# Four graph layers on one core: the memsets between the gathers of layer 0 are taken out

## The chip, the cores and the metric

The kernel runs on one core of one Trainium2 chip. The metric is the device time of one execution in microseconds, the median of several. A profile of one execution lies beside it. A core has engines that run at the same time: TensorE (PE) for matmuls, VectorE (DVE), ScalarE (ACT), GpSimd (POOL) and SyncE (SP), and 16 DMA engines [...].

## The reference

A feature matrix x of 2708 x 512 float32 and an adjacency matrix adj of 2708 x 2708 pass through four layers. Few entries of adj are nonzero: the chance of an edge falls with the row and column number, and the diagonal is set. Every layer ends in a residual and a layernorm. Cut to what matters:

```python
# layer 0: degree-normalised graph convolution
adj_hat = adj + eye
d = 1 / sqrt(adj_hat.sum(axis=1))
x = layernorm(x + (d[:, None] * adj_hat * d[None, :]) @ x @ W.T + b)
# layer 1: adjacency plus a normalised 0/1 mask of it
mask = adj > 0
head = mask / max(sqrt(sum(mask * mask, axis=-1)), eps)
inc = adj + head
x = layernorm(x + (inc @ x) / inc.sum(axis=-1))
# layer 2: attention over the neighbours, gated
# layer 3: x = layernorm(x + relu(adj @ ((x > 0) @ sign(weight).T)))
```

## The kernel before

The function that does the work is `sparse_layers`. Rows are handled in 22 blocks of 128 (the last has 20). Block 0 has neighbours nearly everywhere and uses all of its adjacency row block; every other block uses a few column blocks directly ("direct" tiles) and, for the rest, gathers just those rows that are its neighbours.

The stages, by time in the profile, are these. From 0 to about 187 us the search reads adj, lists the neighbours of every block, packs the adjacency entries (the tiles `a`, fetched by indirect DMA at L1093) and computes y = x W0^T (L1127), which goes to DRAM as `y_rows`. Layer 0 runs from about 187 to 359 us, layer 1 to about 565, layer 2 to about 860 and layer 3 to the end.

Layer 0 is the loop at L1481 over `sequence`, which is 0, 1, 21, 2, 3, ... 20. For a block b it does this:

- DVE adds the bias b0 to the old features (L1486).
- For each gathered tile, `gathered` (L624) issues an indirect DMA on GpSimd (L626) that fetches up to 128 rows of `y_rows` into a buffer `xg`; the pool `s_l0` has ten of them. There are 98 such gathers in the layer.
- PE adds each tile's product with the packed adjacency into a PSUM tile `l0_b` (`add_tile`, L1393). A product of 128x512 float32 shows as two records in the trace. The PSUM pool of these tiles has two buffers.
- `grow1` adds one finished block, the one two places back in the sequence, into block 0's sum for layer 1: two DVE operations build `inc` (L1450, L1453; two buffers), and one matmul (L1454) adds it to `sum1`.
- DVE computes t = sum * dinv + old (L1508), and `layernorm` follows: statistics at L688 to L692, a square root on ACT (L663), Newton steps on DVE (L674 to L683), the normalised row at L704.
- SP writes the block to `x1_rows` in DRAM (L1512), from which layer 1 gathers.

Between the blocks lie side tasks for layer 1: `count_positive` counts positive entries of each block with small matmuls (L1183 to L1187), and `head_steps` turns the counts into the head's values (L1207 to L1226), which are spread by PE transposes (L1231) and copied by ACT (L1239). Blocks are counted in groups, such as 12, 13 and 14.

Layer 1 (from L1640) has the same form and gathers from `x1_rows` through the same function; its first incidence tiles are built at L1674. The search's own gathers have fills of another tile, `s_rest` (L1099), inside a block of code whose order is pinned.

After every third gather of layer 0 and every second of layer 1, `gathered` sets the tile `s_idle` (128x384 float32) to zero on GpSimd (L636). Nothing reads that tile. The table that turns this on is `pause`, keyed by the name of the DRAM tensor. For a tensor in the table, `behind` also adds a dependency without a semaphore from each gather or memset to the one before it, so that the scheduler keeps them in the order of the source. Outside of such pins and of the pinned block of the search, the order of instructions on each engine is set by the scheduler of the kernel language, from the data dependencies and its own costs.

Of the kernel before, what the change touches and what calls it, by code (L numbers as in the profile page):

```python
# [507 lines left out]
def sparse_layers(ctx, tc, x, adj, adj_t, w0_t, b0, w_sa, a_sa, w_gcnb, b_gcnb, wa, ba, wb, bb, w3_t,  # L508
# [56 lines left out]
    y_rows = dram.tile([PAD + P, D], F32, tag="y_rows", name="y_rows")  # L565
    x1_rows = dram.tile([PAD + P, D], F32, tag="x1_rows", name="x1_rows")
# [769 lines left out]
    head_row = heads.tile([P, N], F32, name="s_head_row")  # L1336
    wsa = heads.tile([P, KC, D + EXTRA], F32, name="s_wsa")
    idle = heads.tile([P, 384], F32, name="s_idle")
    for d, every in ((y_rows, 3), (x1_rows, 2)):
        pause[d.tensor.name] = (every, idle)  # L1340
    work = ctx.enter_context(tc.tile_pool(name="s_work", bufs=2, side="right", reuse_waits="tile"))

# [813 lines left out]
def kernel(  # L2156
# [25 lines left out]
    flag = ctx.enter_context(tc.tile_pool(name="flag", bufs=1))  # L2182
    over = flag.tile([1, 1], I32, name="over")
    sparse_layers(tc, *args, over)
    n_over = nc.values_load(over[0:1, 0:1], min_val=0, max_val=-(-x.shape[0] // P))
    with tc.If(n_over > 0):
# [43 lines left out]
```

## Time and profile before

| what | us |
|---|---|
| median of 3 runs | 988.28 |
| lowest, highest | 986.34, 994.11 |
| the profiled execution | 992.0 |
| its span | 990.3 |
| PE busy in the span | 860.8 |
| POOL busy in the span | 549.4 |

The mean granted clock of PE was 0.946 in the profiled execution. The span runs from the first to the last instruction on the core. "Busy" counts work, not waiting or issuing. In a group's line, the part before the bar names source line, engine, operation, output and inputs and count; after the bar stand the busy time, the mean of one in ns, and the idle time of the engine just before them with what ended most of it. Idle time of an engine that others don't wait for costs nothing.

### The profile page before, as it was taken

The page shows a single profiled execution, that of the slowest core. Times are in us where ns is not written, and L with a number is a line of the kernel's source. Part 1 is how long each engine was busy: PE and PEld are TensorE (multiplying, and loading weights), DVE is VectorE, ACT ScalarE, POOL GpSimd, SP SyncE. Part 2 cuts the span into 40 slices and gives each one's busy share as a digit, 9 for nine tenths or more (in the row PEclk, how much of TensorE's full clock was granted, in tenths as well). Part 3 has the DMA queues.
Part 4 walks back from the last instruction along what each step waited for, and adds up shares of the span by engine and source line. Part 5 has one row for each costly group of instructions (what it writes and reads, how often), then busy time and mean ns, then how long its engine had stood idle before and what let it go on. Part 6 is the DMA issues. An engine that isn't in the chain of part 4 may idle for free.

```text
span 990.3 us, 12880 instructions
## 1 busy us (share of the span) xinstructions
PE 860.8 (87%) x3659; PEld 452.2 (46%) x3659; DVE 654.7 (66%) x2538; ACT 381.1 (38%) x822; POOL 549.4 (55%) x660
## 2 busy tenths in 40 slices
PE   1898789759979979999999989988999999599992
PEld 0444344212222324555555634543555555378771
DVE  4888888726657766565654446675888776556685
ACT  2665556100000014554544433333444333254653
POOL 2577888687877647776542054553454320066661
PEclk9998998979989989999999998998999999889996
DMA  9999996466777646777653276786777541299985
GB/s 266 339 336 306 301 310 199 142 193 192 237 211 222 207 132 195 223 220 233 183 176 121 97 249 236 257 276 216 249 274 261 174 149 47 85 316 331 308 249 173
DMA packets 93557, 220.06 MB, mean 222 GB/s; under 512 B 13660, under 2 KB 28364, under 8 KB 93476
## 3 DMA queue, kind: packets, MB, share of 16 engines
q0 software_dynamic: 43008, 127.61, 43.5%
q1 hardware_dynamic: 38520, 76.78, 22.6%
q10 hardware_dynamic: 11948, 14.76, 4.7%
q8 instruction: 31, 0.51, 0.2%
q14 instruction: 50, 0.41, 0.1%
HBM read 178.21 MB, written 31.71 MB: 212 GB/s over the span
## 4 chain that ended last, share of the span: by engine, by line
PE 68%; DVE 14%; DMA 7%; issue 5%; ACT 2%; another core or an unknown queue 2%; POOL 1%; SPq 0%; ACTq 0%; DVEq 0%; POOLq 0%
PE l L1393 17%; PE h L1619 8%; PE e L1844 7%; PE a L1844 7%; PE l L2099 4%; PE pg L1892 4%; PE pc L1892 3%; PE y L1127 3%; PE l L2138 2%; PE l L1454 2%; PE e L1652 2%; PE a L1653 2%; PE px L1953 2%; DVE s_mask L895 2%; DMA xg<-x_rows,i 2%
## 5 line engine op out<-in xcount | busy, mean ns | idle before, releaser
L1093 POOL DMA_INDIRECT a<-in_adj_t_dram,row_at x98 | 111.3, 1136 | 58.7 <-DVE deg L838 26.1
L626 POOL DMA_INDIRECT xg<-x_rows,i x98 | 95.8, 978 | 70.7 <-PE l L1393 37.1
L626 POOL DMA_INDIRECT xg<-y_rows,i x98 | 97.7, 997 | 32.6 <-issue 19.0
L1393 PE MATMUL l<-xg,a 128*32 128x512 f32 (+3 forms) x196 | 86.0, 646 | 12.6 <-DMA xg<-y_rows,i 12.6
L1820 POOL DMA_INDIRECT xg<-x_rows,i x60 | 59.1, 986 | 61.8 <-ACT ae L1575 16.3
L1127 PE MATMUL y<-s_w,xt 128*128 128x512 f32 (+1 forms) x176 | 91.3, 667 | 1.7 <-ACT xt L1119 1.7
L626 POOL DMA_INDIRECT xg<-xw_rows,i x70 | 71.3, 1018 | 38.7 <-issue 15.9
L1820 POOL DMA_INDIRECT a<-x_rows,i x38 | 36.9, 970 | 95.1 <-DVE mask L1578 37.1
L1619 PE MATMUL h<-s_wsa,xt 128*128 128x256 f32 (+3 forms) x352 | 81.9, 385 | 0.0
L1619 PEld LDWEIGHTS h<-s_wsa,xt 128*128 128x128 f32 (+1 forms) x352 | 63.9, 186 | 24.8 <-ACT xt L1614 9.2
L830 ACT ACTIVATE unused<-arow 128x1408 uint8<-128x1408 f32 (+3 forms) x44 | 58.3, 1325 | 3.0 <-DMA x_rows<-s_zero 2.0
L663 ACT ACTIVATE rsqs<-mv 128x1 f32<-128x1 f32 (+2 forms) x56 | 11.3, 202 | 120.7 <-DVE mv L692 58.8
L1844 PE MATMUL a<-xg,a 128*32 128x512 f32 (+2 forms) x120 | 51.2, 629 | 4.3 <-DMA xg<-x_rows,i 4.3
L1127 PEld LDWEIGHTS y<-s_w,xt 128*128 128x128 f32 (+1 forms) x176 | 35.6, 213 | 41.9 <-issue 39.6
L2099 PE MATMUL l<-ws,pw 128*128 128x512 f32 (+1 forms) x210 | 50.8, 394 | 1.7 <-issue 1.2
L1844 PE MATMUL e<-xg,ae 128*32 128x512 f32 (+2 forms) x120 | 47.9, 601 | 1.1 <-issue 1.1
L694 POOL TENSOR_TENSOR rs<-mv,s_neg_half 128x1 f32<-128x1 f32 (+1 forms) x22 | 13.0, 592 | 61.4 <-DVE mv L692 52.0
L1892 PE MATMUL pg<-s_wg,pt 128*128 128x256 f32 (+1 forms) x176 | 45.0, 397 | 1.3 <-ACT pt L1880 1.3
L688 DVE BATCH_NORM_STATS2 st<-t 128x6 f32<-128x512 f32 (+1 forms) x66 | 45.3, 687 | 0.3
L916 PE MATMUL find<-s_sides,s_mask 128*128 128x5 bf16 (+1 forms) x462 | 15.7, 166 | 34.1 <-DVE s_mask L912 25.2
L2099 PEld LDWEIGHTS l<-ws,pw 128*128 128x128 f32 (+1 forms) x210 | 39.4, 190 | 11.9 <-issue 2.9
L1393 PEld LDWEIGHTS l<-xg,a 128*32 128x32 f32 (+3 forms) x196 | 19.8, 146 | 54.4 <-issue 38.6
(307 smaller groups left out, 1995.5 us busy)
## 6 DMA issues: line engine op xcount, KB each, us to landing
arow<-in_adj_dram SPq DMA_DIRECT2D x21, 704.0 KB
arow<-in_adj_dram SPq DMA_DIRECT2D x21, 650.0 KB
x_rows<-f SPq DMA_DIRECT2D x40, 256.0 KB
aw<-in_adj_t_dram SPq DMA_DIRECT2D x21, 320.0 KB
y_rows<-yt ACTq DMA_DIRECT2D x20, 256.0 KB
x_rows<-h SPq DMA_DIRECT2D x19, 257.0 KB
f<-in_x_dram SPq DMA_DIRECT2D x19, 256.0 KB
h_own<-x_rows SPq DMA_DIRECT2D x19, 256.0 KB
```

The costliest lines, as they stand in the source:

```text
L626: nc.gpsimd.indirect_dma_start(out=t, out_offset=None, in_=src[:, :], in_offset=bass.IndirectOffsetOnAxis(ap=index[b][:, i : i + 1], axis=0),)
L688: nc.vector.bn_stats(st[:m], t[:m])
L830: nc.scalar.activation(unused[:m, : ar.shape[1]], ar, AF.Copy, accum_out=row_sums[:m, b, h : h + 1])
L895: nc.vector.tensor_scalar(mask[:m, c0 : c0 + ar.shape[1]], ar, 0.0, None, op0=ALU.not_equal)
L1093: nc.gpsimd.indirect_dma_start(out=packed[b][:, t + len(direct(b)), :], out_offset=None, in_=adj_t, in_offset=bass.IndirectOffsetOnAxis(ap ...
L1127: nc.tensor.matmul(ps[:m], xt[:, k, :m], w0[:, k, :], start=(k == 0), stop=(k == KC - 1))
L1393: nc.tensor.matmul(ps[r0:r1], weights, moving, start=(i == order[0]), stop=last_of(b, i, order))
L1619: nc.tensor.matmul(ps, xt[:, k, :m], w[:, k, :], start=(k == 0), stop=(k == KC - 1))
L1820: nc.gpsimd.indirect_dma_start(out=g, out_offset=None, in_=x2_rows[:, :], in_offset=bass.IndirectOffsetOnAxis(ap=index[b][:, t : t + 1], a ...
L1844: nc.tensor.matmul(ps[r0:r1], weights, moving, start=(i == order[0]), stop=last_of(b, i, order))
L1892: nc.tensor.matmul(ps, pt[:, k, :m], w[:, k, :], start=(k == 0), stop=(k == KC - 1))
L2099: nc.tensor.matmul(whole[b], p[:r, h, b * P : (b + 1) * P], g[:r, :], start=(j == 0 and h == 0), stop=(j == NB - 1 and h == 1),)
```

## The change

One entry of the table goes. The gathers of `y_rows` are then no longer followed by memsets, and they are no longer pinned to each other. The 49 memsets of layer 1 and the 43 of the search stay, and so does the pin on layer 1's gathers.

```diff
     idle = heads.tile([P, 384], F32, name="s_idle")
-    for d, every in ((y_rows, 3), (x1_rows, 2)):
+    for d, every in ((x1_rows, 2),):
         pause[d.tensor.name] = (every, idle)
```

The rest of the program's text is the same. 32 memsets of layer 0 leave the program; the gathers keep their number, their sizes and their buffers.

## The prediction

> **What bounds the kernel now.** I began with the page, to see which engine carries the whole:
>
> ```profile
> span 990.3 us, 12880 instructions
> PE 860.8 (87%) x3659; PEld 452.2 (46%) x3659; DVE 654.7 (66%) x2538; ACT 381.1 (38%) x822; POOL 549.4 (55%) x660
> PE 68%; DVE 14%; DMA 7%; issue 5%; ACT 2%; another core or an unknown queue 2%; POOL 1%; SPq 0%; ACTq 0%; DVEq 0%; POOLq 0%
> L626 POOL DMA_INDIRECT xg<-y_rows,i x98 | 97.7, 997 | 32.6 <-issue 19.0
> ```
>
> The profiled execution took 992.0 us, 1.7 more than its span. TensorE is busy 87% and holds 68% of the chain that ended last; GpSimd, whose work the change takes out, holds 1%. The last line is layer 0's 98 gathers of y rows, which all run on GpSimd. An average says little of one stage, so I cut out layer 0 (196 to 356 us) and asked for the stretch, its chain and its waits:
>
> ```profile
> 196.00:356.00 160.00, 132.56 (x404) 39.27 (x404) 100.40 (x448) 10.28 (x41) 115.28 (x133) 0.90 0.68 203
> ```
>
> The columns are length, then busy time of PE, weight load, DVE, ACT and POOL, then PE clock, DMA share, GB/s. POOL is at 72% (115.28 of 160), PE at 83%, and the DMA engines at 0.68 are not full.
>
> ```profile
> by line: PE l L1393 60.5%; PE l L1454 13.1%; issue 6.3%; DMA xg<-y_rows,i 3.2%; PE hr L1187 2.9%; PE hr L1231 2.6%; DVE t L1508 1.9%; POOL a L1093 1.7%; another core or an unknown queue 1.4%; DVE st L688 1.1%; DVE pos L1185 1.1%; DVE f L704
> ```
>
> In layer 0 too the chain is PE's matmuls (60.5 + 13.1 + 2.9 + 2.6 = 79%). The gathers' transfer is 3.2%, and L626 or L636 on POOL do not appear in the line. The waits (total us, times, longest) say who stands still for whom:
>
> ```profile
> POOL xg L626 <- issue: 19.0, 76, 0.3
> ...
> PE l L1393 <- DMA xg<-y_rows,i: 12.6, 1, 12.6
> ...
> POOL xg L626 <- PE l L1393: 8.7, 13, 2.2
> ...
> PE l L1454 <- DVE t L1508: 4.4, 1, 4.4
> ...
> PE l L1454 <- DVE rsqs L682: 2.3, 1, 2.3
> ```
>
> PE waited for a gather once, for the first one; 97 gathers were there in time. POOL, in turn, waited 13 times for PE to give back one of the ten xg buffers. So GpSimd runs ahead of PE, is stopped by it, and is mostly cover. What stops PE inside the stage is DVE: the sums that `grow1` adds for layer 1 need a normalised block (L1508 to L704).
>
> [...] a gather holds POOL 0.947 us, so fills and gathers share one engine's time. [...] A few gathers take 1.02 to 1.15 us, [...] Here the records of one 128x512 matmul take 0.857 us after a wait (x2 in 2.07 us at 282.79) and 0.427 us otherwise, [...]
>
> **The change part by part.** *The fills.* 32 memsets of s_idle (L636; 15.0 us by the group list, 467 ns each) go. The POOL timeline gives what one costs:
>
> ```profile
> 203.80 0.95 POOL L626 DMA_INDIRECT xg<-y_rows,i  x1 [0.16 <-issue]
> 205.06 0.95 POOL L626 DMA_INDIRECT xg<-y_rows,i  x1 [0.30 <-issue]
> 206.31 0.95 POOL L626 DMA_INDIRECT xg<-y_rows,i  x1 [0.30 <-issue]
> 207.26 0.43 POOL L636 MEMSET s_idle<- 128x384 f32 x1
> 207.85 0.94 POOL L626 DMA_INDIRECT xg<-y_rows,i  x1 [0.16 <-issue]
> ```
>
> Three gathers and a fill take 207.85 − 203.80 = 4.05 us; without the fill they take 3 × 1.25 (206.31 − 205.06) = 3.75 us. A fill costs POOL 0.30 us net, since it sits where a 0.30 us gap would be anyway. 32 × 0.30 = 9.6 us is all that POOL can win, of the 145 us between its first gather (199.6) and its last (344.5).
>
> What of it is on the path? PE's work in the stage is 98 gathered tiles, 18 direct ones and 21 sums, 137 × 2 records × 0.427 = 117 us, and some 9 us of counts and transposes (L1187, L1231). It takes from 204.9 to about 352, so some 21 us are waits and half speed, and only the start is owed to gathers. The first nine gathers contain two fills ahead of tiles that PE takes as they land: 2 × 0.30 = −0.6 us. The other 30 shorten a lead that POOL already has, and POOL turns the time into waiting for buffers. Layer 1 gains nothing there: its first gather needs the last x1 rows written, and POOL stands idle 14.65 us before it.
>
> *The order.* `behind` also fixed the gathers' order for the scheduler. Comparing the order of both programs by engine: gathers and SP's queue come in the same order, and layers 1 to 3 are the same; PE, DVE and ACT are re-sorted inside layer 0. No instruction is added and no new wait. Gather matmuls move ahead of the sums and counts. Step by step:
> - `grow1` of block 1 gets one more matmul (0.86 us) ahead of it, where PE waited 2.3 us for L682: −0.86. `grow1` of block 7 gets three more (2.6 us) where PE waited 4.4 us for L1508: −2.6. Together −3.4.
> - PE ran 2.6 us longer than its work after that second wait, at half speed (282.8 to 288.6). Whether 1.8 us of rest still slows it I can't tell: bounds 0 and −2.6, I take the half, −1.3.
> - The head transposes of blocks 12 to 14 lose cover: four matmuls lie between the last count and them instead of seven (3 × 0.86): +2.6 at most, and I take that, as PE already waited 1.2 us at one such place (L1231 on hd).
> - At the tail the last norm comes seven DVE instructions later, some 0.15 us each: +1.0. One more `grow1` is left for the end; it lies beside the last x1 write and gather, so nothing, and 0.86 us if that cover is gone.
> - DVE's t of two blocks now come in pairs before their norms. Elsewhere PE has 10 to 14 us between a block's last matmul and its sum, 7 to 9 before. More cover: nothing now, since those places didn't wait.
>
> Sum: −0.6 − 3.4 − 1.3 + 2.6 + 1.0 = −1.7 us. The profiled 992.0 becomes 990.3; it stood 3.7 above the median, and I put the difference on the median: 988.28 − 1.7 = 986.6.
>
> **The rivals.**
> *A, POOL paces after all (faster).* If the lead is only apparent, the full 9.6 us come off in place of 0.6: −10.7, 977.6. For: 19.0 us of POOL's idle time is its own issue gap, and PE used the first nine tiles, and again about ten near 260 to 277 us, only 5 to 6.5 us after their issue, when a transfer lands 3.0 to 4.2 us after it. Against: one wait for a gather, 13 for buffers.
>
> *B, the fills let PE's releases through (slower).* In dense gathering PE's semaphore comes late; lines from the timelines of PE and DVE:
>
> ```profile
> 277.26 1.10 PE L1393 MATMUL l<-xg,a 128*128 128x512 f32 x2
> 281.53 0.75 DVE L1508 SCALAR_TENSOR_TENSOR t<-l,s_dinv,f 128x512 f32<-128x512 f32 x1 [2.20 <-remote]
> 282.79 2.07 PE L1454 MATMUL l<-f,inc 128*128 128x512 f32 x2 [4.43 <-DVE t L1508]
> ```
>
> PE ended the block at 278.4; DVE could start on it at 281.5, and PE lost 4.4 us, then half speed. Counting PE's semaphore events that came over 0.06 us after the last matmul's end, I find 38 of 117 in 200–360 (a fill every third gather) and 58 of 96 in 870–970 (layer 3: gathers without fills). If layer 0 goes to layer 3's share (0.60 / 0.32 = 1.86 times), PE's own waits in the stage besides the first, 17.3 us (4.4 + 3.7 + 3.5 + 2.3 + 1.9 + 1.2 + 0.3), grow by 14.9: 986.6 + 14.9 = 1001.5. It decides once they grow by more than the 1.7 us that I give the order. Against it: in layer 3, with the worst share, PE waits 3.0 us in 100; and without fills POOL meets its buffer limit sooner and pauses there, and beside such pauses (231–256, 331–345) few releases were late.
>
> *C, nothing moves,* because the order's terms cancel and the fills were all cover: 988. It lies inside my forecast's own range.
>
> **How the numbers follow.** Forecast (C in it) 0.57, A 0.20, B 0.23. The forecast's own range is 979 to 994: at the low end the start and all gains of the order without its losses (−6.6) and a third of A's other fills (−3.0), at the high end the two losses alone (+3.6) and 2 us for the distance of the median from its neighbours. The 8-in-10 range takes in A with 3 us for its spread below, and B up to its point: 974 to 1001. About 1% (9.9 us) is what a measurement of this kernel can tell from no change. A at 977.6 is just past it, so 0.6 of A and a little of the forecast's tail and spread: faster 0.18. B is mostly past it, with a little of the tail: slower 0.20. Same 0.62.
>
> **What would show it.** Right: gathers 1.25 us apart with no fills, more POOL time lost to PE (from 8.7 to 15 or more), last x1 norm within 3 us of before, the wait at `grow1` of block 7 under 2 us, layer 1 onwards shifted and unchanged. A shows as a layer 0 shorter by 8 us or more and few buffer waits. B shows as more L1508 and L1454 waits, more half-clock stretches in layer 0, and DVE released microseconds after PE's last matmul. I am wrong if layer 0 moves by more than 8 us either way, or if layers 1 to 3 change, which neither the order nor the buffers explain.

## The result and the profile after

The changed kernel took 999.06 us (median of 21 runs, 992.34 to 1009.01) against 992.51 us for the kernel before in the same series: a ratio of 1.008, 95% interval 1.0061 to 1.0100. I had forecast a gain of 1.7 us; the change lost 6.6 us by the medians and about 8 by the ratio, which is another estimate of the same. The time lies in my range and the change within 1%, but the sign is that of rival B.

Where the time went, in the two profiled executions (992.0 and 1006.26 us; the second lies 7.2 above its median, so this pair shows more than the medians do):

| stretch, read from the GpSimd timeline | before | after |
|---|---|---|
| start to first gather of `y_rows` | 199.6 | 202.2 |
| from there to the last gather's end | 144.8 | 149.8 |
| first `y_rows` gather to first `x1_rows` gather (layer 0) | 159.5 | 171.5 |
| from there to the first gather of layer 3 | 508.2 | 507.3 |
| from there to the end | 122.9 | 123.7 |

Layer 0 holds 12 of the 14 us. Five of them had passed when the last gather ended; the other seven came after it, as PE was then further behind: its last product of a gathered tile ended 13.7 us after the last gather, 7.8 us in the kernel before. The page of the changed kernel:

```profile
span 1004.5 us, 12849 instructions
PE 862.2 (86%) x3659; PEld 455.1 (45%) x3659; DVE 655.0 (65%) x2538; ACT 380.6 (38%) x822; POOL 533.3 (53%) x628
PE 65%; DVE 13%; DMA 7%; issue 6%; another core or an unknown queue 5%; ACT 3%; POOL 1%; ACTq 0%; SPq 0%; DVEq 0%; POOLq 0%
L626 POOL DMA_INDIRECT xg<-y_rows,i x98 | 96.0, 980 | 54.0 <-issue 21.3
```

The matrix work is the same, and POOL is busy for 16 us less. But its idle time ahead of the gathers grew from 32.6 to 54.0 us, and "another core or an unknown queue" has 5% of the chain where it had 2%. There is one core, so this is a wait whose releaser the profile couldn't tell. The cut at 196 to 356 us shows PE less busy (118.83 us, it was 132.56) and slower (clock 0.85, it was 0.90):

```profile
196.00:356.00 160.00, 118.83 (x375) 36.49 (x375) 88.15 (x389) 7.78 (x34) 100.68 (x103) 0.85 0.66 205
```

The waits of layer 0 (to 372 us, since it ends later; total us, times, longest) name the place:

```profile
DVE pos L1185 <- remote: 36.2, 4, 20.4
...
PE hr L1187 <- DVE pos L1185: 27.0, 4, 10.4
POOL xg L626 <- PE l L1393: 14.1, 13, 3.6
...
POOL xg L626 <- remote: 12.8, 7, 3.7
PE l L1393 <- DMA xg<-y_rows,i: 11.9, 2, 10.9
...
PE hr L1187 <- issue: 2.0, 1, 2.0
...
PE l L1454 <- DVE inc L1453: 1.7, 2, 1.0
...
PE l L1454 <- DVE f L704: 1.1, 1, 1.1
```

PE stood 27.0 us before the counting matmuls (L1187), in four waits for the tile `pos`. The same lines of the kernel before:

```profile
PE hr L1187 <- issue: 3.5, 4, 1.2
...
PE hr L1187 <- DVE pos L1185: 1.9, 2, 1.7
```

What the view names as the end of such a wait can shift between `pos` and "issue", so I also give the sum before the counts: 29.0 us against 5.4. DVE, which makes `pos`, stood 36.2 us itself for something "remote". The timelines of PE, DVE and POOL around the longest case:

```profile
214.86 0.34 PE L1187 MATMUL hr<-valid,pos 128*128 128x1 bf16 x8
...
218.14 0.32 PE L1231 MATMUL hr<-s_ident,hd 128*128 128x128 f32 x1
226.13 0.21 PE L1187 MATMUL hr<-s_sides,pos 128*128 128x1 bf16 x2 [7.67 <-DVE pos L1185]
...
225.38 0.69 DVE L1185 TENSOR_SCALAR pos<-a 128x1024 bf16<-128x1024 f32 x1 [20.43 <-remote]
...
219.75 0.95 POOL L626 DMA_INDIRECT xg<-y_rows,i  x1 [0.30 <-issue]
221.00 0.95 POOL L626 DMA_INDIRECT xg<-y_rows,i  x1 [0.30 <-issue]
225.66 1.23 POOL L626 DMA_INDIRECT xg<-y_rows,i  x1 [3.71 <-remote]
```

PE counted the block before with `pos` by 215.20. `pos` has one buffer, so DVE must know that before it writes the next block's. It learnt it at 225.38, 10.2 us later. In between PE ran out of work (from 218.5) and GpSimd out of buffers (from 221.95), and all three went on within a microsecond. The trace also lists semaphore events, the signals of an engine for which instructions of others wait: those of PE stop at 214.9, and then five come at once from 225.36 to 225.52. Until it met its own buffer limit GpSimd had issued gathers 1.25 us apart with nothing between; the events came 3.4 us after it had stopped.

So two things may have come together: PE's events held back, and an order in which PE stands behind one buffer. The experiments take them apart.

### The profile page after: what moved, and what is told of

It is laid out like the page before. It is cut to its first block, busy times and chain, and to the rows that moved or that the text cites. A ratio compares the mean times of both kernels' runs of the same rounds, so it can differ in the third digit from the quotient of the medians.

```text
span 1004.5 us, 12849 instructions
## 1 busy us (share of the span) xinstructions
PE 862.2 (86%) x3659; PEld 455.1 (45%) x3659; DVE 655.0 (65%) x2538; ACT 380.6 (38%) x822; POOL 533.3 (53%) x628
## 4 chain that ended last, share of the span: by engine, by line
PE 65%; DVE 13%; DMA 7%; issue 6%; another core or an unknown queue 5%; ACT 3%; POOL 1%; ACTq 0%; SPq 0%; DVEq 0%; POOLq 0%
PE l L1393 14%; PE h L1619 8%; PE e L1844 6%; PE a L1844 6%; PE l L2099 4%; PE pg L1892 4%; PE l L2138 3%; PE pc L1892 3%; PE y L1127 3%; DMA xg<-x_rows,i 2%; PE e L1652 2%; PE a L1653 2%; PE l L1454 2%; DMA arow<-in_adj_dram 2%
## 5 line engine op out<-in xcount | busy, mean ns | idle before, releaser
L1393 PE MATMUL l<-xg,a 128*32 128x512 f32 (+3 forms) x196 | 85.3, 660 | 12.4 <-DMA xg<-y_rows,i 11.9
L1393 PEld LDWEIGHTS l<-xg,a 128*32 128x32 f32 (+3 forms) x196 | 20.1, 151 | 55.9 <-issue 37.4
```

The lines of the kernel that those rows point to most:

```text
L1393: nc.tensor.matmul(ps[r0:r1], weights, moving, start=(i == order[0]), stop=last_of(b, i, order))
```

## The experiments

The runs of one letter share a chip and a series of the kernel before on it. In the table, "latest event" is the longest time from the end of PE's last signalling instruction to a semaphore event of PE during layer 0, in the profiled execution; "layer 0" runs from the first gather of `y_rows` to the first of `x1_rows`, there too. Both are of one execution for each row, while the ratios are of many. The chips differ: on one of them (runs e1 to e4, the kernel before at 964.9 us) PE's events in layer 0 were prompt in all four profiles; on the others (the kernel before at 991.6 to 1000.6 us) they came late. I call them the prompt chip and the late chips; which one a series ran on was not chosen, and the kernel before has a profile from a late chip alone.

| run | fills of layer 0 | order of PE, DVE, ACT | ratio to before, interval | latest event, us | layer 0, us |
|---|---|---|---|---|---|
| before, late chip | every 3rd | old | 1 | 6.0 | 159.5 |
| changed, late chip | none | new | 1.008, 1.0061–1.0100 | 9.7 | 171.5 |
| e1, prompt | none | old | 0.9899, 0.9876–0.9923 | 0.1 | 140.9 |
| e2, prompt | every 3rd | new | 1.0031, 1.0014–1.0048 | 0.1 | 152.1 |
| e3, prompt | none, two `pos` | scheduler's | 0.9921, 0.9898–0.9945 | 0.1 | 143.2 |
| e4, prompt | small, every 3rd | scheduler's, near the new | 0.9994, 0.9979–1.0008 | 0.1 | 148.6 |
| f1, late | none (changed kernel) | new | 1.0142, 1.0076–1.0208 | 5.7 | 165.2 |
| f2, late | none | old | 1.0032, 1.0008–1.0057 | 6.4 | 164.9 |
| f3, late | every 3rd | new | 1.0064, 1.0034–1.0095 | 8.7 | 165.0 |
| f4, late | none, two `pos` | scheduler's | 1.0042, 1.0017–1.0067 | 7.3 | 165.7 |
| g1, late | every gather | old | 1.0086, 1.0061–1.0110 | 0.1 | 168.9 |
| g2, late | long, every 3rd | old | 1.0170, 1.0122–1.0219 | 0.1 | 178.3 |
| g3, late | every 3rd, two `pos` | scheduler's | 0.9995, 0.9969–1.0020 | 7.5 | 163.6 |
| g4, late | none (changed kernel) | new | 1.0080, 1.0051–1.0109 | 10.0 | 167.3 |
| h1, late | small, every gather | old | 1.0022, 0.9998–1.0046 | 6.6 | 161.5 |
| h2, late | half, every gather | old | 0.9983, 0.9960–1.0006 | 1.6 | 156.1 |
| h3, late | every 2nd | old | 0.9941, 0.9919–0.9964 | 2.6 | 158.3 |
| h4, late | none (changed kernel) | new | 1.0093, 1.0055–1.0131 | 9.5 | 170.8 |

**Fills and order apart (e1, e2, f2, f3).** The order of one kernel is pinned on the other by chaining layer 0's instructions on PE, DVE and ACT, with dependencies that cost no semaphore. In the traces PE's instructions then come in exactly the order that was meant, and DVE's too as far as the records go. The lists of places are left out here:

```diff
+L0_ORDER = (
...
     l0_ps.close()
+    for places in L0_ORDER:
+        for p0, p1 in zip(places, places[1:]):
+            tc.add_manual_dep(
+                l0_mine[p1], l0_mine[p0].name,
+                mybir.DependencyInfo(mybir.DependencyClass.NoSync, mybir.DependencyReason.DATA),
+                reason="l0_order",
+            )
```

> The fills are out as in the change, but the instructions of PE, DVE and ACT in layer 0 are pinned to the order that they have in the kernel before. Theory H (without fills PE's semaphore events are held back while gathers are issued back to back, whatever the order): 1.004 to 1.012 of before, with at least two stretches in layer 0 in which PE's events stay out for 4 us or more and come in a burst. Theory O (the new order is the cost: it puts counts where PE stands still until the single pos buffer comes free): 0.990 to 1.001 of before, PE's wait on pos L1185 below 4 us in all.

> The fills stay as before, but PE, DVE and ACT are pinned in layer 0 to the order of the changed kernel. Theory H: 0.996 to 1.002 of before, PE's wait on pos L1185 below 8 us in all (it is 27.0 in the changed kernel), no event of PE later than about 4 us. Theory O: 1.005 to 1.012, with PE's wait on pos above 15 us. If both fills and order are needed, e1 and e2 both lie within 0.997 to 1.003.

On the prompt chip theory O had e1 right and theory H had not: with the old order, taking the fills out wins 1.0%, 8.8 us by the medians. e2 fell between the two expectations: with the fills in, the new order costs 0.3%. Theory H could not be tested there, since no event was held in either run. The profiles say how the fills' time came off: from the first gather to the end of the last took 128.4 us in e1 and 137.1 in e2. On a late chip the pair was run again, beside the changed kernel:

> The changed kernel once more. In the profiles of the four runs so far no event of PE came more than 0.1 us after its matmul, and before took 964.9 us instead of 992.5: another chip. If PE's events are late here too: 1.006 to 1.010 of before, with PE waiting over 15 us for pos L1185. If they are not: 0.994 to 1.002, as e4 (the same order with fills that fit in the gap) had 0.9994, with no event held.

> The fills out, the old order pinned, again, beside the changed kernel on one chip. If PE's events are prompt: 0.988 to 0.992 as in e1, so that the order alone costs the difference to the changed kernel. If they are late: theory H says 1.003 or more; theory O says below 1.000 with less wait on pos than in the changed kernel.

> The fills kept, the new order pinned, again. With prompt events: 1.001 to 1.005 as in e2. With late ones: theory H 0.998 to 1.003, theory O 1.006 or more.

Now both parts cost: taking out the fills alone +0.32% (f2), the order alone +0.64% (f3). Their product, 1.0032 x 1.0064 = 1.0096, lies among what the changed kernel had in four series (1.008, 1.0142, 1.0080, 1.0093); on this chip it had 1.0142, from four executions and with a wide interval, above what I expected of f1. f2 and e1 are one program, and differ in sign: 1.0032 against 0.9899. In f2 the hold that was shown above is there with the old order too:

```profile
225.01 0.69 DVE L1242 TENSOR_SCALAR pos<-a 128x1024 bf16<-128x1024 f32 x1 [19.58 <-remote]
...
226.00 0.95 POOL L683 DMA_INDIRECT xg<-y_rows,i  x1 [3.33 <-remote]
```

(The table of places moves the lines by 57: L1242 is `pos`, L683 the gather.) So without fills events came late in both orders on this chip (6.4 us at most in f2, 5.7 in f1), as H said, and the new order adds its own cost (+0.64% in f3), as O said. Neither theory alone holds; f3 also shows that the fill after every third gather doesn't keep events prompt, with one 8.7 us late (6.0 in the kernel before).

The old order has long waits before the counts too, once the fills are out. In f2:

```profile
PE hr L1244 <- issue: 7.0, 2, 6.4
...
PE hr L1244 <- DVE hd L1274: 5.8, 1, 5.8
...
PE hr L1244 <- DVE rsqs L739: 2.5, 1, 2.5
...
PE hr L1244 <- DVE pos L1242: 0.8, 1, 0.8
```

That is 16.1 us, where the kernel before had 5.4. By the same sum f3, with fills and the new order, has 11.7, and the changed kernel 29.0, 20.3 (f1), 20.0 (g4) and 27.3 (h4). On the prompt chip e1 has 0.6 and e2, with the new order pinned, none. So this wait comes with the held events, in either order, and the new order makes it longer. Where f2 and f3 lost their time the profiles don't settle: layer 0 took 164.9 to 165.7 us in all of f1 to f4, and the stages that the change doesn't touch differ by several us between these executions. h1 and h4 below make a clearer pair on one chip. Both have gathers 1.25 us apart (h1's fills fit in the gap), h1 with the old order and h4 with the new: 1.0022 against 1.0093, layer 0 at 161.5 us against 170.8, and 18.2 us before the counts against 27.3.

**A second `pos` buffer (e3, f4, g3).**

```diff
-                pos = pool.tile([P, max(ROOM) + 2, P], BF16, tag="pos", name=f"pos{b}", bufs=1)
+                pos = pool.tile([P, max(ROOM) + 2, P], BF16, tag="pos", name=f"pos{b}", bufs=2)
```

> The changed kernel with two pos buffers instead of one, so that DVE can make the next block's pos while PE's release of the last one is outstanding. If the wait of PE on pos is the whole cost (27.0 us there, against 1.9 before): 0.980 to 0.995 of before. Theory H with other readers of the late events behind it (t of the block, xg buffers): 0.998 to 1.006, with the time turning up as waits for t L1508 or for buffers.

> The changed kernel with two pos buffers, again. With prompt events: 0.990 to 0.994 as in e3. With late ones: 0.985 to 0.998 if pos alone carried the wait, 1.000 or more if the late events find another reader.

> The kernel before, fills and all, with two pos buffers. DVE then makes the next block's pos without PE's event on the last. On either kind of chip 0.990 to 1.000: where events are late PE's waits on pos go (1.9 us here), where they are prompt the fills still hold GpSimd.

With two buffers the changed kernel falls to about the level that it has with the old order: 0.9921 beside e1's 0.9899 where events are prompt, 1.0042 beside f2's 1.0032 where they are late. This doesn't show that the one buffer is what the order costs. The scheduler re-sorts layer 0 once more for two buffers, on PE and still more on DVE, so the order of e3 and f4 is neither the old nor the new; two buffers with a pinned order were not run. On the late chip the held events then found another reader, as the second expectation had it. The waits of f4:

```profile
DVE t L1508 <- remote: 34.8, 3, 20.7
...
PE l L1393 <- DVE t L1508: 8.1, 1, 8.1
PE hr L1187 <- DVE pos L1185: 6.7, 1, 6.7
```

DVE's wait moved from `pos` to t, and PE's from 15.4 us on `pos` in f1, on the same chip, to 6.7 there and 8.1 on t; its layer 0 is no shorter (165.7 us, 165.2 in f1). With the fills in, the second buffer shows no gain (g3, 0.9995), also with an order of its own.

**Pauses and held events (e4, g1, g2, h1, h2, h3).** e4 writes 128x8 in place of 128x384; the others pin the old order and change the width or the spacing of the fills:

```diff
-    for d, every in ((y_rows, 3), (x1_rows, 2)):
+    for d, every in ((y_rows, 1), (x1_rows, 2)):
-            nc.gpsimd.memset(idle, 0.0)
+            nc.gpsimd.memset(idle[:, :8] if src is y_rows else idle, 0.0)
```

(This is h1. g1 has the first edit alone; h2 has `:192`, h3 has 2 in place of 1, g2 keeps 3 and has an `idle` of 1536.)

> The fills of layer 0 write 128x8 instead of 128x384; the scheduler then gives PE the order of the changed kernel. If a pause of GpSimd in time is what lets PE's events through: as the changed kernel, 1.004 to 1.012 of before, since such a fill takes about 0.1 us and fits in the gap of 0.30. If any other instruction between the gathers is enough: 0.996 to 1.002, with PE's wait on pos below 8 us.

e4 could not decide that question, as the chip held no event. It shows something else: with in effect no fills, on the prompt chip, 0.9994. PE's order is nearly that of the changed kernel, DVE's is another one. By its waits PE stood for gathers nine times there, where the kernel before on the late chip had once:

```profile
PE l L1393 <- DMA xg<-y_rows,i: 15.3, 9, 9.2
```

Beside e1, with the old order on the same chip, layer 0 is 7.7 us longer (148.6, 140.9). PE waited for `pos` 0.6 us in e1 and not at all in e4, so on this chip the order's cost is no wait of PE on `pos`. All of PE's idle time in the layer grew only from 17.1 to 19.2 us; its busy time grew from 128.7 to 133.9 for the same matmuls, at a mean clock of 0.93 in place of 0.96. Which of the moved instructions does it is open.

> The kernel before with a fill after every gather of layer 0 in place of every third, PE, DVE and ACT pinned to their order of before. A gather with its fill then takes about 0.95 + 0.43 + 0.16 = 1.54 us of GpSimd instead of 1.35 on average: 98 x 0.19 = 19 us more for GpSimd. If pauses between the gathers are what lets PE's events through on a chip where they come late: fewer events held over 2 us than in the runs with a fill every third gather, and a time of 0.995 to 1.008 there, PE now waiting for gathers. If the pauses don't matter for the events: as many held, and 1.005 to 1.02. Where events are prompt: 1.008 to 1.02.

> The kernel before with layer 0's fills four times as wide (128x1536, about 1.6 us, still every third gather), the order of before pinned. GpSimd's cycle of three gathers becomes about 5.2 us, 170 us in all, so GpSimd sets the stage: 1.015 to 1.03 of before. If an event held back comes out whenever GpSimd pauses for 1.5 us or more, no event is later than about 4.5 us (the cycle) and the late ones come out during fills. If pauses don't matter, holds of 5 us and more stay.

Both g1 and g2 fell on a late chip, and in layer 0 of both not one event came more than 0.1 us after its instruction, where the changed kernel on the same chip (g4, expected at 1.006 to 1.016 and found at 1.0080) had 10.0. So the theory that pauses don't matter for the events falls. g1's time, 1.0086, is just above the range for it, as GpSimd now set the pace: its waits for buffers are nearly gone, and PE waits for gathers 31 times.

```profile
PE l L1450 <- DMA xg<-y_rows,i: 28.1, 31, 12.1
...
POOL xg L683 <- PE l L1450: 3.2, 20, 0.2
```

PE's clock in g1's layer 0 was 0.98. Between these and no fill lie shorter pauses:

> The kernel before with a fill of 128x8 after each gather of layer 0, the order of before pinned. e4 shows that such a fill (0.12 us) fits into the gap between two gathers, so GpSimd issues as fast as without fills. If the presence of another instruction lets PE's events through, no event is late and the time is 0.985 to 0.995 of before. If it is the time of the pause, on a chip with late events: holds of 5 us and more, 1.000 to 1.008. On a chip with prompt events: 0.988 to 0.994 as in e1.

> The same with 128x192 after each gather, some 0.25 us: a gather with its fill takes about 1.36 us, the average of the kernel before, evenly spread. Late events and time of the pause: fewer holds than before, 0.990 to 1.003. Prompt events: 0.996 to 1.004.

> The same with the full fill of 128x384 after every second gather: 1.40 us for a gather. Late events: fewer holds than with every third, none of 5 us, 0.990 to 1.004. Prompt events: 1.002 to 1.008.

> The changed kernel. Late events: 1.006 to 1.014. Prompt events: 0.996 to 1.002, and its PE waits in layer 0 are for gathers and pos, with no event later than 0.1 us.

The timeline of POOL in h1 shows why its fills cost nothing and help nothing: the memset sits inside the gap, and a gather still follows the last one by 1.25 us, until POOL stands on a held event.

```profile
215.08 0.95 POOL L683 DMA_INDIRECT xg<-y_rows,i  x1 [0.18 <-issue]
216.03 0.12 POOL L693 MEMSET s_idle<- 128x8 f32 x1
216.33 0.96 POOL L683 DMA_INDIRECT xg<-y_rows,i  x1 [0.18 <-issue]
...
221.38 0.95 POOL L683 DMA_INDIRECT xg<-y_rows,i  x1 [2.73 <-remote]
```

Its latest event was 6.6 us, as without fills (f2, 6.4). At a gather in 1.38 us on average (h2) the latest was 1.6, at 1.40 (h3) it was 2.6, at 1.54 (g1) 0.1. So on these chips another instruction between the gathers wasn't enough; events came earlier where there was more time between them. The average isn't all of it either: with the fill after every third gather it is 1.35 us, little below h2's 1.38, and events were 6.0 to 8.7 us late (before, f3, g3). How evenly the pauses lie may count, but the order, the chip and the number of fills differ there too. A pause without a memset was not run. h3, 0.9941, is the one version that was clearly faster than the kernel before on a late chip; on the prompt one it wasn't run, and e1 says that fills cost there. The changed kernel wasn't run on the prompt chip either; e4 is the nearest.

## Why the prediction was wrong, point by point

Two steps failed. The fills were put down as cover whose loss costs nothing, although PE's events came later still without them (9.7 us at most in the changed kernel's profile, 6.0 in that of the kernel before); and the new order was said to bring "no new wait". In their place the pinned runs on a late chip show +0.32% for the fills alone and +0.64% for the order alone, and PE's idle time before the counts went from 5.4 to 29.0 us.

- *A fill costs GpSimd 0.30 us net, 9.6 us in all.* Right: gathers follow at 1.25 us without fills.
- *Of these only 0.6 us is on the path.* This step failed on the prompt chip: e1 won 8.8 us there, nearly the whole 9.6 of rival A. I had PE's work at 126 us and never set it against GpSimd's own: 98 gathers at 4.05 / 3 us are 132. GpSimd was the longer of the two. That PE's waits for held events hid this on the late chip, and that I read them as GpSimd's lead, is how I explain it now; no run tests it.
- *GpSimd turns the won time into waiting for buffers.* Right on a late chip: it waited 14.1 us for L1393 and 12.8 us for "remote", after 8.7.
- *The order wins 3.4 us at two sums and 1.3 us of half speed.* The waits at L1454 did fall, from 8.6 us (4.4 + 2.3 + 0.3, and 1.6 behind the cut at 356 us) to 3.5 us (1.7 + 1.1 + 0.7). But the step priced the waits that could be seen and put the counts of L1187 at nothing. Their wait on the one `pos` buffer was 1.9 us, and all of PE's idle time before them 5.4. With the fills out that became 16 to 18 us in the old order and 20 to 29 in the new. The half-speed term has the wrong sign too, as PE's clock in the cut fell from 0.90 to 0.85. In the kernel before the clock was 0.50 to 0.56 in the first 2 to 5.8 us after PE's waits of 12.6, 3.7, 2.3 and 4.4 us in layer 0; it was also 0.50 from 334 to 336 us, 2.5 us after a wait of 1.7 us had ended.
- *The head transposes cost 2.6 us, the tail 1.0.* The first didn't come: no wait of PE at L1231 is left. The second did: the last norm ended 5.1 us after the last gathered product, 4.0 before.
- *Rival B.* That events come later without fills is what the profiled pair shows (9.7 us at most against 6.0); of the other runs of the changed kernel g4 and h4 had 10.0 and 9.5, f1 5.7. PE's waits in layer 0 besides the first gather went from 18.9 us (17.3 and the 1.6 behind the cut) to 33.8 (27.0 + 2.0 + 1.7 + 1.1 + 1.0 + 0.7 + 0.3), +14.9. That I had priced +14.9 is luck: part of it is the order's, and I let the share of late events grow, which it didn't (36 of 115 in layer 0 against 39 of 117). What grew is how late they are, 113.8 us in sum against 36.5.
- *My argument against B,* that GpSimd would meet its buffer limit and pause there: it does, but in the case shown the events came out 3.4 us after that, when PE had stood for some 7 us and the event that DVE needed was 10.2 us late.
- *Layers 1 to 3 unchanged.* Right, 507.3 and 123.7 us against 508.2 and 122.9. My sign of being wrong, a layer 0 that moves by more than 8 us, came true in the profiled pair (12.0).

## What to carry to other kernels

When instructions are taken out or re-sorted, list for every engine the single-buffered tiles, since there one engine stands until it hears from another, and ask what a late signal would cost, even where the wait seen is small: 1.9 us on `pos` became 27.0. When a schedule changes as a side effect, pin the old order once on the new program and the new order on the old one; that took the two costs apart here. Before calling an engine cover, set its own work in the stage against that of the engine said to bound it, since waits of the latter can hide that the two are nearly equal. And measure on more than one chip where the change is about 1%: the same program was 1.0% faster on one and 0.3% slower on another.

## What the runs showed of the hardware

While GpSimd issued indirect gathers 1.25 us apart, PE's semaphore events came up to 10.0 us late in layer 0 on the late chips (g4), PE going on meanwhile with whatever was not waiting (from 214.9 to 218.5 us in the case shown). There the held ones arrived in one burst 3.4 us after the end of GpSimd's last gather; two others of the same profile came at 267.2 us, 9.7 us late, 1.7 us after the end of a gather. With the old order, a gather in 1.54 us (g1), or a fill of 128x1536 after every third (g2), some 1.4 us by my estimate from the 0.12, 0.27 and 0.43 us that 8, 192 and 384 columns took, left none later than 0.1 us. From the end of PE's signalling instruction to the event it was thus 0.1 us or less in some runs and up to 10.0 in others. On one chip the gathers without fills held nothing in layer 0 (0.1 us at most in e1, where the same program had 6.4 on a late chip in f2), and the kernel before took 964.9 us there against 991.6 to 1000.6 elsewhere. Why the chips differ, and where the events wait, no run here shows.
